# First attention: the triangle of the diagonal score blocks selected by GpSimd in SBUF instead of added by mask products in PSUM

## The chip, the cores and the metric

The kernel runs on one core of one Trainium2 chip, as one launch. The metric is the device time in microseconds of one execution; several runs are taken and their median is given. The core has five engines with a queue each that work side by side: TensorE (PE in the profile, with its weight loads listed apart as PEld), VectorE (DVE), ScalarE (ACT), GpSimd (POOL) and SyncE (SP, which here only starts DMAs). TensorE writes its results into PSUM, a small memory of eight banks; ScalarE and VectorE read them from there, and GpSimd works in SBUF, the large on-chip memory.

## The reference

The kernel computes one transformer block with two attentions and two feed-forward parts on 1024 tokens of 512 channels, in float32. The change concerns the first attention alone: 32 heads of 16 channels, rotary positions, a causal mask, and a softmax over all earlier tokens.

```python
def attention_fwd(x, wq, wk, wv, wo, n_heads=32):
    B, T, C = x.shape                       # 1, 1024, 512
    hd = C // n_heads
    xq = (x @ wq.T).reshape(B, T, n_heads, hd)
    xk = (x @ wk.T).reshape(B, T, n_heads, hd)
    xv = (x @ wv.T).reshape(B, T, n_heads, hd)
    xq = rotary_pos_emb(xq)
    xk = rotary_pos_emb(xk)
    scores = jnp.einsum('bqhd,bkhd->bhqk', xq, xk) * hd ** (-0.5)
    causal = jnp.tril(jnp.ones((T, T), dtype=bool))
    scores = jnp.where(causal[None, None], scores, NEG_INF)
    probs = jax.nn.softmax(scores.astype(jnp.float32), axis=-1).astype(xq.dtype)
    out = jnp.einsum('bhqk,bkhd->bqhd', probs, xv).reshape(B, T, C)
    return out @ wo.T

x = x + attention_a(layernorm(x))
x = x + ffn(layernorm(x))
x = x + attention_b(layernorm(x))
x = x + ffn(layernorm(x))
```

## The kernel before

The first attention lies between about 70 and 372 us of the span, after the projections of queries, keys and values. Heads are padded to 32 rows, so that four heads share the 128 partitions: one group of four heads is called a column `c` here, and there are eight (`NCA`). `qT` and `kT` hold queries and keys with channels on partitions. A score matmul of one head uses only 32 rows of the PE array, so that the matmuls of four heads can run in it at once.

For each column of heads the scores are made twice.

- **Row scores** (`row_scores`, L358): tile `s`, queries on partitions, keys along the free axis. They serve only to find each query's maximum: `maxima` (L375 and L378, VectorE) reduces them to the negated maximum, with a mask for the diagonal block added in the same instruction. `with_maxima` (L393, L397) turns the negated maxima and writes them by DMA (SP's queue) into an extra row of `qT`, where a row of ones in `kT` meets them.
- **Column scores** (`col_scores`, L407): tile `sT`, keys on partitions, queries along the free axis. Because of the extra row they come out of the matmul with the query's maximum already taken off, so that no allowed score is above zero. `exponentials` (L429, ScalarE) takes the exponential from PSUM to the SBUF tile `p`. `product` (L449) multiplies `p` with the values (and a column of ones, which yields the sums of the softmax) into the PSUM tile `oT`. `normalize` (L486 to L508) copies it out, and with several DMAs and one GpSimd multiply (L508) divides by the sums.

The work advances in steps. In step `n` of column `c`, `step` makes the column scores of column `c` and the row scores of column `c + 1`, half a step at a time: the first half takes the column scores of heads 2 and 3 with the row scores of heads 0 and 1, the second half the other way round. So each half has four score tiles. After the scores of a half come `maxima`, `exponentials`, the call `due()`, and half of the product of the step two before. A column has nine steps. The last column (`c` = 7) has no next one, and its ten steps take all four heads' column scores at once.

A step covers one score tile of 512 columns per head, put together from blocks. The blocks on the diagonal of the causal mask, where half of the entries must vanish, are gathered four at a time: `diagonal(qc)` is a list of four blocks of 128 keys by 128 queries. Each of the first seven columns has two such triangle steps, its steps 4 and 7; the last has steps 0 and 7. So there are 16 triangle steps, 14 of them in two halves. In these, `exponentials` first adds a mask of 0 and a huge negative number to the four triangles in PSUM: for each head four matmuls (L427) of a slice of the identity `identb` with the bfloat16 mask `maskT`, spread over the four blocks by a broadcast. The exponential then makes zeros of the masked entries.

Score tiles of both kinds share one PSUM pool of seven banks (`a_s`, tag `s`); the eighth is `oT`. The tiles `p` have five buffers. `later` is a list of deferred pieces of work with a count; `due()`, called once in each half-step (twice in a step of the last column), counts each down and runs those that fall below zero. Before, only `normalize` uses it, for the inversion of the sums and for L508.

The order of instructions on each engine isn't quite that of the source: a scheduler in the framework places them by its own estimate and by priorities, and assigns the buffers. Each engine then works through its queue in that order, and a waiting instruction holds up those behind it. DMAs of the first attention are issued on SP's queue; GpSimd's queue also issues some early weight loads (`midway`).

Of the kernel before, what the change touches and what calls it, by code (L numbers as in the profile page):

```python
# [10 lines left out]
BF16 = mybir.dt.bfloat16  # L11
AF = mybir.ActivationFunctionType
ALU = mybir.AluOpType
# [3 lines left out]
P = 128  # L17
# [4 lines left out]
QC = 512  # L22
# [3 lines left out]
NEG = -(2.0**100)  # L26
# [12 lines left out]
B = 32  # L39
# [25 lines left out]
class Block:  # L65
# [207 lines left out]
    def attend_a(self, ctx_pool, pt, work, ps_s, ps_o, qT, kT, v_p, project_qk, project_v, midway, tail):  # L273
        nc, tc = self.nc, self.tc
        HC = P // PADA
        with ExitStack() as ctx:
            cp = ctx.enter_context(tc.tile_pool(name="a_c", bufs=1))
# [7 lines left out]
            mask = cp.tile([P, QC], BF16, tag="mask", name="mask")  # L285
            nc.gpsimd.memset(mask, 0.0)
            nc.gpsimd.affine_select(
                out=mask, in_=mask, compare_op=ALU.is_ge, fill=NEG, base=QC - P, pattern=[[-1, QC]], channel_multiplier=1
            )
            identb = cp.tile([P, P], BF16, tag="identb", name="identb")  # L290
            make_identity(nc, identb)

            maskT = cp.tile([P, P], BF16, tag="maskT", name="maskT")
            nc.gpsimd.memset(maskT, 0.0)
            nc.gpsimd.affine_select(
                out=maskT, in_=maskT, compare_op=ALU.is_ge, fill=NEG, base=0, pattern=[[1, P]], channel_multiplier=-1
            )

# [7 lines left out]
            def diagonal(qc):  # L308
                return [(qc, 4 * qc + a, a * P, (a + 1) * P) for a in range(4)]
# [26 lines left out]
            def rows_of(j):  # L336
                return slice(j * PADA, (j + 1) * PADA)
# [11 lines left out]
            def col_pieces(c, n):  # L349
                return list(placed(by_cols(c)[n], lambda qc, b, x0, x1: x1 - x0))  # L350
# [48 lines left out]
            def col_scores(c, n, heads, made):  # L399

                pieces = col_pieces(c, n)
                masked = pieces[0][:4] in diagonal(pieces[0][0])
                for j in heads:
                    made[j] = ps_s.tile([P, QC], F32, tag="s", name=f"sT{c}_{n}_{j}")
                for x, (qc, b, x0, x1, at, end) in enumerate(pieces):
                    for j in heads:
                        nc.tensor.matmul(  # L407
                            made[j][:, at:end],
                            lhsT=kT[rows_of(j), c, b * P : (b + 1) * P],
                            rhs=qT[rows_of(j), c, qc * QC + x0 : qc * QC + x1],  # L410
                            start=x == 0,
                            stop=x == len(pieces) - 1 and not masked,
                        )
                        yield

            def exponentials(c, n, heads, made, p):
                pieces = col_pieces(c, n)
                end = pieces[-1][-1]

                if pieces[0][:4] in diagonal(pieces[0][0]):  # L420
                    mask = maskT.unsqueeze(1).to_broadcast([P, len(pieces), P])
                    for j in heads:

                        for a in range(P // B):
                            rows = slice(a * B, (a + 1) * B)
                            to = made[j][rows, :].rearrange("p (a k) -> p a k", k=P)
                            nc.tensor.matmul(to, lhsT=identb[:, rows], rhs=mask, start=False, stop=True)  # L427
                for j in heads:
                    nc.scalar.activation(p[:, j, :end], made[j][:, :end], AF.Exp)  # L429

            def product(c, n, p):

# [90 lines left out]
            later = []  # L523
# [10 lines left out]
            def step(rc, cc, n):  # L534
# [8 lines left out]
                for half in range(2 if both else 1):  # L543
                    rows, cols = (2 * half, 2 * half + 1), (2 - 2 * half, 3 - 2 * half)
                    if not both:
                        rows = cols = range(HC)
                    gens = []
                    if cc is not None:
                        gens.append(col_scores(cc, n, cols, madeT))
                    if rc is not None:  # L550
                        gens.append(row_scores(rc, n, rows, made))
                    drain(gens)
                    if rc is not None:
                        maxima(rc, n, rows, made)
                    if cc is not None:
                        exponentials(cc, n, cols, madeT, p)
                    due()
                    if not both:
                        due()
                    next(turns, None)  # L560
# [935 lines left out]
```

## Time and profile before

| | |
|---|---|
| Median of 3 runs | 1570.31 us (1570.02 to 1570.70) |
| The profiled execution's own time | 1571.58 us |
| Its span (first to last instruction) | 1569.8 us |
| Mean granted TensorE clock | 0.999 |
| Triangle mask products L427 | 256, from 132.3 to 365.3 us |
| Exponentials L429 | 292, from 120.6 to 370.4 us |
| First matmul of the output projection L1370 | 371.5 us |

A row of a costly group names the line, the engine, the operation, output and input tiles with their shapes and the count; after the bar stand the busy time in us that the group covers and the mean ns of one, and after the second bar how long the engine was idle just before them and what ended that idle time. In a listing in order of time the columns are the start in us, the duration in us, then engine, line, operation, tiles and shapes, and how many such instructions follow each other; a bracket gives the idle time before. A float32 matmul of these sizes shows as two passes. Matmuls overlap, and their ends are modelled, so that sums of PE time count overlapping parts twice where they are not given as covered time. In a table of stretches each engine's busy time is followed by the number of its instructions; then come the granted clock as a share of full speed, the busy share of the DMA engines, and GB/s.

### The profile page before, as it was taken

The numbers are of one execution on the slowest core, as the hardware profiler recorded it, in microseconds if no ns is written. First come the engines' busy times: TensorE is split into PE (matmuls) and PEld (weight loads), VectorE is DVE, ScalarE is ACT, GpSimd is POOL, SyncE is SP. The second block draws the span as 40 slices with busy tenths as digits, with TensorE's granted clock in tenths as the row PEclk, the third lists the DMA queues.
The fourth block names the chain that finished last, engine by engine and source line by source line (L and its number), as shares of the span: only waits on it lengthen the run. The fifth ranks groups of instructions, "written<-read, shape, count | busy, mean of one in ns | idle before, by whom it ended". The sixth has DMA issues, their size and how long they took to land.

```text
span 1569.8 us, 32216 instructions
## 1 busy us (share of the span) xinstructions
PE 1543.4 (98%) x12894; PEld 926.1 (59%) x12894; DVE 1058.7 (67%) x2537; ACT 662.1 (42%) x1597; POOL 463.1 (29%) x571
## 2 busy tenths in 40 slices
PE   9999999999999999999999999999999999999998
PEld 5545455555555657557656755755765675556654
DVE  4557778773566886666776667766676766776753
ACT  2216666665223544443434444343343444433430
POOL 3000000002233433432443343334244333333450
PEclk9999999999999999999999999999999999999999
DMA  5000222220033102412330331241133032135001
GB/s 208 1 1 6 20 22 19 18 20 19 29 99 95 42 1 68 68 42 55 63 60 28 82 38 31 65 72 41 54 62 61 28 69 35 34 86 122 4 2 54
DMA packets 80950, 75.34 MB, mean 48 GB/s; under 512 B 14944, under 2 KB 56672, under 8 KB 80800
## 3 DMA queue, kind: packets, MB, share of 16 engines
q1 hardware_dynamic: 70272, 52.56, 14.3%
q0 software_dynamic: 8848, 17.58, 7.7%
q10 hardware_dynamic: 1680, 3.15, 0.5%
q8 instruction: 101, 1.65, 0.5%
q14 instruction: 49, 0.40, 0.1%
HBM read 33.08 MB, written 18.87 MB: 33 GB/s over the span
## 4 chain that ended last, share of the span: by engine, by line
PE 84%; DVE 7%; POOL 4%; ACT 2%; issue 2%; SPq 0%; DMA 0%; DVEq 0%; ACTq 0%; POOLq 0%
PE s L1079 13%; PE wo L765 12%; PE o L1140 11%; PE sT L407 8%; PE pq L993 8%; PE kv L920 5%; PE oT L449 5%; PE pm_f L714 3%; PE or L1140 3%; PE s L358 3%; PE pj_v L218 2%; PE pj_q L218 2%; PE pm_ao L1370 2%; PE pj_k L218 2%; DVE p L1081 2%
## 5 line engine op out<-in xcount | busy, mean ns | idle before, releaser
L1091 POOL TENSOR_SCALAR p<-p,rs 128x1024 f32<-128x1024 f32 (+7 forms) x256 | 192.8, 754 | 407.0 <-DVE rs L1090 406.3
L1079 PE MATMUL s<-kT,qT 128*128 128x512 f32 (+3 forms) x768 | 297.0, 496 | 10.9 <-DVE p L1081 10.9
L1079 PEld LDWEIGHTS s<-kT,qT 128*128 128x128 f32 x768 | 137.9, 190 | 174.7 <-issue 114.4
L765 PE MATMUL wo<-wo,oT 128*128 128x512 f32 x512 | 237.9, 593 | 1.0 <-ACT spare L781 1.0
L1106 DVE STREAM_TRANSPOSE pT<-p 128x512 f32<-128x512 f32 (+3 forms) x256 | 152.9, 602 | 109.5 <-PE o L1140 58.8
L1088 ACT ACTIVATE p<-p,nm 128x1024 f32<-128x1024 f32 (+7 forms) x256 | 198.3, 775 | 17.9 <-ACT nm L1086 0.4
L429 ACT ACTIVATE p<-sT 128x512 f32<-128x512 f32 (+1 forms) x292 | 155.2, 593 | 89.8 <-PE s L358 35.2
L1085 DVE TENSOR_REDUCE nm<-p 128x1 f32<-128x1024 f32 (+7 forms) x256 | 188.2, 735 | 2.9
L1140 PEld LDWEIGHTS o<-pT,va 32*128 32x128 f32 x4212 | 172.9, 185 | 21.7 <-issue 10.4
L1086 ACT ACTIVATE nm<-nm 128x1 f32<-128x1 f32 x256 | 51.6, 202 | 315.6 <-DVE nm L1085 314.7
L1140 PE MATMUL o<-pT,va 32*128 32x224 f32 (+5 forms) x4212 | 181.3, 324 | 0.8 <-DVE pT L1106 0.8
L358 PE MATMUL s<-kT,qT 32*128 32x512 f32 (+3 forms) x768 | 164.4, 520 | 0.0
L407 PE MATMUL sT<-qT,kT 32*128 32x128 f32 (+3 forms) x1152 | 155.3, 401 | 0.3 <-DMA qT<-negT 0.3
L765 PEld LDWEIGHTS wo<-wo,oT 128*128 128x128 f32 x512 | 94.2, 190 | 90.7 <-issue 78.8
L1081 DVE SCALAR_TENSOR_TENSOR p<-s,rq,relr 128x512 f32<-128x512 f32 x192 | 120.9, 646 | 9.9 <-PE s L1079 9.7
L993 PE MATMUL pq<-xnTb,wq 128*128 128x512 f32 x240 | 117.8, 600 | 0.4
L1081 DVE SCALAR_TENSOR_TENSOR p<-s,rq,rel 128x512 f32<-128x512 f32 (+1 forms) x192 | 102.5, 558 | 21.0 <-PE s L1079 20.9
L407 PEld LDWEIGHTS sT<-qT,kT 32*128 32x128 f32 x1152 | 80.6, 184 | 50.6 <-issue 29.4
L1112 DVE STREAM_TRANSPOSE tT<-p 128x512 f32<-128x512 f32 (+3 forms) x128 | 63.7, 498 | 57.0 <-POOL p L1091 30.6
L375 DVE TENSOR_REDUCE part<-s 128x1 f32<-128x512 f32 x128 | 81.6, 684 | 28.1 <-PE s L358 20.1
L1090 DVE RECIPROCAL rs<-ss 128x1 f32<-128x1 f32 x256 | 39.8, 155 | 85.9 <-ACT p L1088 82.1
L508 POOL TENSOR_TENSOR o<-o,over 64x512 f32<-64x512 f32 x12 | 15.3, 1272 | 270.1 <-DMA o<-oTs 224.0
(201 smaller groups left out, 2161.8 us busy)
## 6 DMA issues: line engine op xcount, KB each, us to landing
va<-v SPq DMA_DIRECT2D x256, 64.0 KB
xd<-beside POOLq DMA_DIRECT2D x56, 256.0 KB, 4.1
wq<-in_b_WqT_dram SPq DMA_DIRECT2D x8, 1024.0 KB
wo<-in_b_WoT_dram SPq DMA_DIRECT2D x8, 1024.0 KB
x_x<-in_x_dram SPq DMA_DIRECT2D x8, 256.0 KB
wkv<-in_b_WkT_dram SPq DMA_DIRECT2D x8, 256.0 KB
xd<-x_x ACTq DMA_DIRECT2D x8, 256.0 KB
wkv<-in_b_WvT_dram SPq DMA_DIRECT2D x8, 256.0 KB
```

The costliest lines, as they stand in the source:

```text
L358: nc.tensor.matmul(made[j][:, at:end], lhsT=qT[rows_of(j), c, i * P : (i + 1) * P], rhs=kT[rows_of(j), c, kc * QC : kc * QC + end - at], s ...
L407: nc.tensor.matmul(made[j][:, at:end], lhsT=kT[rows_of(j), c, b * P : (b + 1) * P], rhs=qT[rows_of(j), c, qc * QC + x0 : qc * QC + x1], st ...
L429: nc.scalar.activation(p[:, j, :end], made[j][:, :end], AF.Exp)
L765: nc.tensor.matmul(ps, lhsT=oTs[g, h][:, t * P : (t + 1) * P], rhs=wo[:, h, :], start=(h == heads[0]), stop=(h == heads[-1]))
L993: ins = nc.tensor.matmul(ps, lhsT=w[:, kc, :], rhs=x[:, kc, :], start=first and kc == 0, stop=kc == H - 1, skip_group_check=True,)
L1079: nc.tensor.matmul(s, lhsT=qT[:, i * P : (i + 1) * P], rhs=kT[:, lo:hi], start=True, stop=True)
L1081: nc.vector.scalar_tensor_tensor(p[:, lo:hi], s, rq[:, i : i + 1], rels[i % 2][:, at + lo : at + hi], ALU.mult, ALU.add)
L1085: nc.vector.tensor_reduce(nm, p[:, :w], AX.X, ALU.max, negate=True)
L1088: nc.scalar.activation(p[:, :w], p[:, :w], AF.Exp, bias=nm, scale=slope, accum_out=ss)
L1091: nc.gpsimd.tensor_scalar(p[:, :w], p[:, :w], rs, 1.0, ALU.mult, ALU.mult)
L1106: nc.vector.transpose(PT[:, i : i + (NT - 1) * (m - 1) + 1 : NT - 1, :], p[:, : m * P].rearrange("p (j k) -> p j k", k=P))
L1140: nc.tensor.matmul(cols(o[:, a], j, j + skip), lhsT=vs[g][j // 4][rows, j % 4 * NB + b, :], rhs=moving(j, j + skip, rows, slice(b * B, (b ...
```

## The change

The mask products go, with `identb` and `maskT`. In a triangle step the scores leave PSUM by ScalarE as max(-s, 0) (`Relu` with scale -1) into `p`. GpSimd's `affine_select` then keeps the entries on and above the diagonal in SBUF and fills the others with the huge positive number, over both heads of the half (128 x 1024) or all four heads in the last column (128 x 2048). The exponential with scale -1 is taken in place in SBUF, as a deferred piece of work: its count is 1 for head 2 and 2 for the others, so that `due()` runs it in the next half-step or the one after. Steps without triangles are as before.

```diff
-            identb = cp.tile([P, P], BF16, tag="identb", name="identb")
-            make_identity(nc, identb)
-
-            maskT = cp.tile([P, P], BF16, tag="maskT", name="maskT")
-            nc.gpsimd.memset(maskT, 0.0)
-            nc.gpsimd.affine_select(
-                out=maskT, in_=maskT, compare_op=ALU.is_ge, fill=NEG, base=0, pattern=[[1, P]], channel_multiplier=-1
             )
...
             def col_scores(c, n, heads, made):
 
                 pieces = col_pieces(c, n)
-                masked = pieces[0][:4] in diagonal(pieces[0][0])
...
-                            stop=x == len(pieces) - 1 and not masked,
+                            stop=x == len(pieces) - 1,
...
             def exponentials(c, n, heads, made, p):
                 pieces = col_pieces(c, n)
                 end = pieces[-1][-1]
 
-                if pieces[0][:4] in diagonal(pieces[0][0]):
-                    mask = maskT.unsqueeze(1).to_broadcast([P, len(pieces), P])
+                if pieces[0][:4] not in diagonal(pieces[0][0]):
                     for j in heads:
-
-                        for a in range(P // B):
-                            rows = slice(a * B, (a + 1) * B)
-                            to = made[j][rows, :].rearrange("p (a k) -> p a k", k=P)
-                            nc.tensor.matmul(to, lhsT=identb[:, rows], rhs=mask, start=False, stop=True)
+                        nc.scalar.activation(p[:, j, :end], made[j][:, :end], AF.Exp)
+                    return
+
+
                 for j in heads:
-                    nc.scalar.activation(p[:, j, :end], made[j][:, :end], AF.Exp)
+                    nc.scalar.activation(p[:, j, :], made[j], AF.Relu, scale=-1.0)
+                lo, hi = min(heads), max(heads) + 1
+                of = p[:, lo:hi, :].rearrange("p j (a k) -> p (j a) k", k=P)
+                nc.gpsimd.affine_select(
+                    out=of,
+                    in_=of,
+                    compare_op=ALU.is_ge,
+                    fill=-NEG,
+                    base=0,
+                    pattern=[[0, (hi - lo) * (QC // P)], [1, P]],
+                    channel_multiplier=-1,
+                )
+                for j in heads:
+                    of = p[:, j, :]
+                    later.append([1 if j == 2 else 2, lambda of=of: nc.scalar.activation(of, of, AF.Exp, scale=-1.0)])
```

## The prediction

> **What bounds the kernel now.** I read the page's engine table, then busy time by stretch, then the first attention's costliest groups, then one triangle step in order of time, then GpSimd's rows by shape, and last the granted clock.
>
> ```profile
> PE 1543.4 (98%) x12894; PEld 926.1 (59%) x12894; DVE 1058.7 (67%) x2537; ACT 662.1 (42%) x1597; POOL 463.1 (29%) x571
> ```
>
> TensorE (PE) is busy almost throughout. A stretch inside the first attention (times are us from the span's start):
>
> ```profile
> 250.00:300.00 50.00, 50.00 (x684) 25.06 (x680) 39.86 (x110) 31.18 (x58) 3.81 (x3) 1.00 0.26 22
> ```
>
> The columns are PE, PEld, DVE, ACT, POOL, clock: PE 50.00 of 50, ScalarE (ACT) 31.18, GpSimd (POOL) 3.81. So PE sets the pace, ACT has a third of its time free, and POOL is nearly empty. What the change touches, between 80 and 520 us:
>
> ```profile
> L429 ACT ACTIVATE p<-sT 128x512 f32<-128x512 f32 (+1 forms) x292 | 155.2, 593 | 89.8 <-PE s L358 35.2 <-PE sT L427 32.5 <-PE sT L407 21.6
> L427 PE MATMUL sT<-maskT,identb 128*32 128x512 bf16 x256 | 19.3, 384 | 0.0
> ```
>
> The 256 mask products cover 19.3 us of PE. One triangle step (column 4, first triangle), PE and then ACT:
>
> ```profile
> 262.98 0.37 PE L407 MATMUL sT<-qT,kT 32*128 32x128 f32 x1
> ...
> 263.55 0.60 PE L407 MATMUL sT<-qT,kT 32*128 32x128 f32 x7
> 264.08 0.61 PE L427 MATMUL sT<-maskT,identb 128*32 128x512 bf16 x8
> 264.52 0.61 PE L449 MATMUL oT<-p,v_p 128*32 128x256 f32 x8
> 265.06 0.37 PE L407 MATMUL sT<-qT,kT 32*128 32x128 f32 x1
> ...
> 268.87 0.58 PE L407 MATMUL sT<-qT,kT 32*128 32x384 f32 x1
> ...
> 269.10 0.58 PE L358 MATMUL s<-kT,qT 32*128 32x384 f32 x1
> ...
> 270.73 0.48 PE L407 MATMUL sT<-qT,kT 32*128 32x256 f32 x1
> ```
>
> ```profile
> 264.59 1.09 ACT L429 ACTIVATE p<-sT 128x512 f32<-128x512 f32 x2 [1.21 <-PE sT L427]
> 266.70 1.08 ACT L429 ACTIVATE p<-sT 128x512 f32<-128x512 f32 x2 [1.02 <-PE sT L427]
> ```
>
> Triangle half-steps start at 262.98 and 265.06, the two halves of the next step at 267.23 and 268.87, the step after at 270.73. The masks delay the products by 264.52 - 264.08 = 0.44. ACT idles 1.0 to 1.2 before each pair.
>
> **What goes.** 28 batches of 8 masks at 0.44 and two of 16 at 0.87 (364.61 to 365.48 in the last column) are 12.3 + 1.8 = 14.1 us of PE's queue; 19.3 counts overlap with neighbours. That is the whole possible gain. The setup of `identb` and `maskT` (POOL, about 1 us near 6 to 11 us) goes too; I count nothing, since PE is 47.78 of 50 busy there behind loads and layer norm, and at most 1 us if it led.
>
> **What comes.** Relu replaces Exp at the PSUM exit, one for one; the same 128x512 ACT instruction is taken at L429's 0.60 (a copy, L486, takes 0.593). 64 Exps in place are new: two back to back occupy 1.08, so one follows another after 0.49. Bounds for an in-place Exp: 0.49 to 0.72 (L1088, 128x512 in SBUF, with a bias and a sum, 722 ns). I take 0.49, as these have neither. POOL gains 28 selects of 128x1024 and two of 128x2048, shapes the trace lacks. Its nearest rows:
>
> ```profile
> L105 POOL TENSOR_SCALAR_AFFINE_SELECT rel<-rel 128x512 f32<-128x512 f32 x2 | 1.4, 742 | 0.0
> masks.py:199 POOL TENSOR_SCALAR_AFFINE_SELECT ident<-ident 128x128 f32<-128x128 f32 x1 | 0.3, 282 | 0.0
> L1091 POOL TENSOR_SCALAR p<-p,rs 128x1024 f32<-128x1024 f32 x32 | 36.0, 1126 | 74.6 <-DVE rs L1090 74.6
> L508 POOL TENSOR_TENSOR o<-o,over 64x512 f32<-64x512 f32 x12 | 15.3, 1272 | 270.1 <-DMA o<-oTs 224.0 <-DMA over<-over 39.0 <-DMA qT<-negT 7.0
> ```
>
> The select itself: (742 - 282)/384 = 1.20 ns per element, so 0.74 + 512 x 1.20 = 1.35 at 1024 and 2.57 at 2048. Below: 1.13 (L1091). Above: L508's 2.48 ns per element, 2.54. Handing from POOL to ACT and back costs 0.12 together: at 378.04 POOL ends `mb_f`, ACT's 0.81 (L149) follows, at 378.97 POOL goes on. One round trip ACT, POOL, ACT is S = 1.35 + 0.12 = 1.47 (1.25 to 2.66).
>
> The Trainium skill (GPSIMD Engine Reference, section 3.1) gives 1.8 cycles per element at 1.2 GHz for a tight loop: by estimate 1.54 at 1024, which would add 28 x 0.19 = 5 us to the sum below.
>
> **Where the Exps stand.** The source defers them by half a step, but a scheduler lays the instructions out. In the changed program as built, ACT's queue at all 14 paired triangles reads: Relu of heads 2, 3; Exp 2, 3; Relu 0, 1; Exp 0, 1; then the next step. Each first Exp waits for a select that starts only after the Relus before it. Behind the wait on ACT's queue stand the second half's Relus and the next step's Exps, and PE waits for those, because seven PSUM banks serve all scores. As built, the fourth score matmul of the next step's second half (the one at 269.10) waits for the bank that the next step's first Exp frees (in 13 of 14 triangles; in the other a neighbour does). Its start, with 262.98 as zero: Relu starts at 1.19 (last score matmul ends 263.55 + 0.60, 0.02 to wake ACT); two Relus 1.09; S 1.47; two Exps 0.98; two Relus 1.09; S 1.47; two Exps 0.98; the next step's first Exp 0.60; 0.05 to wake PE: 8.92. From there to the step after takes 270.73 - 269.10 = 1.63: 10.55. The 14 stretches of before last 7.65 to 8.32, mean 7.77, masks included. Net 2.78 each, **38.9 us**; PE has no slack to regain it.
>
> POOL's queue: L508 stands ahead of each column's first triangle and in six columns runs across it (264.38 to 265.65, while the first select is ready at 264.17 + 1.09 + 0.08 = 265.34). It delays that select 0.2 to 0.7, together **2.6**. The DMAs of L508 and SP's queue keep their places; the 12 multiplies behind a select are needed only by the output projection. DVE keeps its instructions; at 40 of 50 it waits with PE. L508's own duration stays 1.27 to 1.28 in all 12 beside a busy DVE, so no slowdown between these two is counted.
>
> Last column (four heads at once). First triangle: Relus from 349.35 (the scores' end) on take 3 x 0.49 + 0.60 = 2.07, select 2.57 + 0.12, two Exps 0.98, four Exps of the next step 1.96, the other two Exps 1.09 (so the built order): 358.14; the products that need them take 1.08, so the next scores come at 359.2, not 355.50: +3.7. Second: the same chain from 364.65 ends at 373.44, and the last products (369.17 to 371.49, 2.32) end at 375.76: +4.3. **8.0 us**; the mask saving is inside.
>
> **The clock.** The second wait leaves PE empty: `sT1` may start at the end of the second Relu pair (1.19 + 1.09 + 1.47 + 0.98 + 1.09 = 5.82) and runs 0.58, so from 6.4 to 8.92, 2.5 us. The trace shows once what such a gap may do:
>
> ```profile
> 492.07:495.48 3.41, 1.54 (x11) 0.35 (x9) 2.01 (x3) 1.61 (x2) 0.00 (x0) 1.00 0.41 101
> 556.92:560.33 3.41, 1.65 (x14) 0.65 (x12) 3.22 (x9) 1.96 (x4) 1.49 (x2) 1.00 0.00 0
> 560.33:563.75 3.42, 3.42 (x11) 1.87 (x8) 2.61 (x9) 2.41 (x6) 1.65 (x1) 0.50 0.00 0
> ```
>
> After 3.41 us with PE 1.65 busy the granted clock was 0.50 for 3.42; after one with 1.54 it stayed. Each drop costs PE half of 3.42, 1.7. A gap of 2.5 against windows of 3.41 at any phase lies whole within one, which leaves at most 0.9 busy, in (3.41 - 2.5)/3.41, some 3 of 10 cases; of 16 gaps I take five: **8.5** (bounds 0 and 27).
>
> The Trainium skill (TensorE: Matmul & The Clock Gate, section on HAM oscillation) sets the danger at idle gaps above some 3.4 us; by it there would be no drop here and the sum would be 8.5 lower. The row at 560.33, after a gap of 1.60, differs.
>
> **The sum.** The profiled execution took 1571.58 (span 1569.8 and 1.8 around it), 1.27 above the median 1570.31. 1571.58 + 38.9 + 2.6 + 8.0 + 8.5 = 1629.6; less 1.27, **1628**.
>
> **Rivals.**
> - *Waits without clock drops* (1.54 busy once did no harm): 1628.3 - 8.5 = 1620; with the select at its lower bound, 28 x 0.22 less, 1613.
> - *A drop after nearly every gap*: 16 x 1.7 = 27, so 1647.
> - *A slow select* at L508's rate: 28 x 1.19 + 2 x 2.5 = 38 on top, 1666 with the drops. For it: L508 is slower per element; against: L105 is the same operation.
> - *Faster*: the gain stands because the waits stay off PE. ACT has 19 of 50 us free, and if the Exps really ran half a step late, four half-steps would hold 12 ACT instructions, 5.9 us against 4 x 1.64 = 6.6. Price: all of the 14.1, 1556. It decides if the round trip fits into ACT's idle 1.0 to 1.2 before each pair. S + 0.98 = 2.45 does not, and the built order doesn't defer. That is also where the change does not do what its source says.
>
> **Chances.** Forecast 0.47, no drops 0.25, many drops 0.10, slow select 0.09, faster 0.07, no change 0.02. The range 1606 to 1650 leaves out the faster cases and the slow select. About 0.2% is what a measurement here tells from no change: faster 0.07, same 0.02, slower 0.91.
>
> **What would show it.** L427 gone; ACT idle 1.4 to 1.5 before an Exp, released by POOL, about 30 times; select at 1.35; triangle start to the step after next 10.5; PE idle some 2.5 released by ACT; the first attention longer by some 50, all else unchanged; clock 0.50 in a few 3.4 us stretches. Wrong if the Exps don't wait, or PSUM holds PE up less than the built waits say.

## The result, and the profile after

| | before | after |
|---|---|---|
| Median | 1570.51 us (4 runs, 1570.02 to 1572.17) | 1650.88 us (4 runs, 1643.93 to 1654.85) |
| Ratio | | 1.0505, 95% interval 1.0465 to 1.0545 |
| The profiled execution's own time | 1571.58 us | 1653.68 us |
| Mean granted TensorE clock | 0.999 | 0.971 |
| First matmul of the output projection | 371.49 us | 454.88 us |

The changed kernel is 5% slower. The profiled execution is 82.1 us longer, and all of it arises in the first attention: its end comes 83.4 us later, and what follows takes 1.3 us less.

Line numbers move with the change: column scores are L398, row scores L350, Exp out of PSUM L413, Relu L418, the select L421, Exp in place L432, the product L452, GpSimd's multiply L511, the maxima L367 and L370.

From the page of the changed kernel: the engine table's first line, the granted clock in 40 slices (41.3 us each) and the group of the row scores.

```profile
PE 1594.6 (97%) x12638; PEld 939.8 (57%) x12638; DVE 1059.0 (64%) x2537; ACT 695.1 (42%) x1661; POOL 496.5 (30%) x597
...
PEclk9998888889899999999999999999999999999999
...
L350 PE MATMUL s<-kT,qT 32*128 32x512 f32 (+3 forms) x768 | 203.4, 588 | 25.5 <-ACT p L413 25.4
```

PE has 256 matmuls fewer and is busy 51 us longer. That can't be more work. The clock row shows one reason: slices 4 to 9 and 11, in the first attention, stand at 8. And the row scores now wait 25.4 us for ScalarE.

The stretch that was shown of before, in the same columns (PE, PEld, DVE, ACT, POOL, clock):

```profile
250.00:300.00 50.00, 46.17 (x504) 21.50 (x504) 30.90 (x92) 28.57 (x54) 6.84 (x6) 0.86 0.18 13
```

PE now has idle time here (3.83 of 50, none before), at a clock of 0.86 instead of 1.00, and does 504 matmuls instead of 684. ScalarE is busy for 28.57 us of the 50, less than the 31.18 before: it isn't the bound either. One triangle step, half after half, in ScalarE's queue in order of time (the idle time ahead and what ended it stand in brackets):

```profile
262.93 1.08 ACT L418 ACTIVATE p<-sT 128x512 f32<-128x512 f32 x2 [0.89 <-PE s L350]
265.41 1.15 ACT L432 ACTIVATE p<-p 128x512 f32<-128x512 f32 x2 [1.39 <-POOL p L421]
266.46 1.06 ACT L418 ACTIVATE p<-sT 128x512 f32<-128x512 f32 x2
268.72 1.15 ACT L432 ACTIVATE p<-p 128x512 f32<-128x512 f32 x2 [1.19 <-POOL p L421]
269.77 1.06 ACT L413 ACTIVATE p<-sT 128x512 f32<-128x512 f32 x2
```

and GpSimd's queue beside it:

```profile
263.07 1.26 POOL L511 TENSOR_TENSOR o<-o,over 64x512 f32<-64x512 f32 x1 [21.71 <-DMA o<-oTs]
264.29 1.08 POOL L421 TENSOR_SCALAR_AFFINE_SELECT p<-p 128x1024 f32<-128x1024 f32 x1
267.60 1.09 POOL L421 TENSOR_SCALAR_AFFINE_SELECT p<-p 128x1024 f32<-128x1024 f32 x1 [2.22 <-ACT p L418]
```

Relu, wait, Exp, Relu, wait, Exp: the Exp that the source defers stands directly behind the Relus of its own half, and ScalarE sits idle 1.39 and 1.19 for GpSimd. Only at 269.77 can it empty a bank for the next step. TensorE's matmuls and, in the last line, its weight loads:

```profile
267.58 0.91 PE L398 MATMUL sT<-qT,kT 32*128 32x384 f32 x2
270.40 0.62 PE L350 MATMUL s<-kT,qT 32*128 32x384 f32 x1 [1.92 <-ACT p L413]
...
272.03 1.08 PE L452 MATMUL oT<-p,v_p 128*32 128x256 f32 x8
```

```profile
270.40 0.18 PEld L350 LDWEIGHTS s<-kT,qT 32*128 32x128 f32 x1 [2.53 <-ACT p L413]
```

PE is empty for 1.92 us, its loader for 2.53, until that bank is free. Then the product of the next lines takes 1.08 where a product of the same eight matmuls took 0.61 before. The windows of the granted clock around this gap (the last but two column is the clock):

```profile
263.99:267.40 3.41, 3.41 (x49) 1.92 (x47) 2.63 (x11) 2.02 (x5) 1.39 (x2) 1.00 0.25 13
267.40:270.82 3.42, 1.50 (x13) 0.60 (x10) 0.86 (x6) 2.23 (x5) 1.09 (x1) 1.00 0.84 26
270.82:274.23 3.41, 3.41 (x27) 1.91 (x26) 1.71 (x8) 1.10 (x3) 1.27 (x1) 0.50 0.02 1
274.23:277.64 3.41, 3.41 (x44) 2.00 (x36) 1.59 (x8) 1.09 (x2) 0.00 (x0) 0.50 0.02 5
277.64:281.06 3.42, 3.42 (x68) 2.31 (x62) 2.99 (x13) 2.17 (x4) 0.00 (x0) 1.00 0.00 0
```

After the window with the gap (PE 1.50 of 3.42), two whole windows run at half clock, although PE is shown busy throughout in both. The trace has 15 such stretches between 141 and 455 us, 13 of them two windows long, 95.6 us at half clock together.

Two costs, then: a wait and a slower clock. A triangle's length, from its start to the start of the step after next, is 7.77 on average before. The first triangle after the change, which ends just as the first half-clock stretch begins (141.1), takes 10.28; the others but one take 11.1 to 12.6 (the exception, 8.34, is column 6's first, where PE's gap is only 0.50). The excess of the 14 is 49.3, the last column's 12.6, and the other 21 to 22 lie mostly in half-steps behind the triangles that run at the low clock.

### The profile page after: what moved, and what is told of

It is laid out like the page before. It is cut to its first block, busy times and chain, and to the rows that moved or that the text cites. A ratio compares the mean times of both kernels' runs of the same rounds, so it can differ in the third digit from the quotient of the medians.

```text
span 1651.9 us, 31785 instructions
## 1 busy us (share of the span) xinstructions
PE 1594.6 (97%) x12638; PEld 939.8 (57%) x12638; DVE 1059.0 (64%) x2537; ACT 695.1 (42%) x1661; POOL 496.5 (30%) x597
## 4 chain that ended last, share of the span: by engine, by line
PE 58%; DVE 7%; POOL 3%; ACT 2%; issue 2%; DVEq 0%; ACTq 0%; POOLq 0%
PE s L1082 12%; PE wo L768 11%; PE o L1143 10%; PE pq L996 7%; PE kv L923 5%; PE pm_f L717 3%; PE or L1143 3%; PE pm_ao L1373 2%; DVE p L1084 2%; POOL p L1094 2%; DVE pT L1109 1%; PE st L1060 1%; DVE nm L1088 1%; ACT p L1091 1%; DVE oT L1192 1%
## 5 line engine op out<-in xcount | busy, mean ns | idle before, releaser
L350 PE MATMUL s<-kT,qT 32*128 32x512 f32 (+3 forms) x768 | 203.4, 588 | 25.5 <-ACT p L413 25.4
L398 PE MATMUL sT<-qT,kT 32*128 32x128 f32 (+3 forms) x1152 | 192.4, 451 | 4.4 <-ACT p L413 4.4
L413 ACT ACTIVATE p<-sT 128x512 f32<-128x512 f32 (+1 forms) x228 | 120.5, 589 | 83.0 <-PE s L350 62.2
L398 PEld LDWEIGHTS sT<-qT,kT 32*128 32x128 f32 x1152 | 93.9, 205 | 65.9 <-issue 31.4
L350 PEld LDWEIGHTS s<-kT,qT 32*128 32x128 f32 x768 | 85.4, 211 | 48.9 <-ACT p L413 34.4
L367 DVE TENSOR_REDUCE part<-s 128x1 f32<-128x512 f32 x128 | 81.8, 686 | 43.0 <-PE s L350 37.7
L452 PE MATMUL oT<-p,v_p 128*32 128x128 f32 (+1 forms) x1552 | 106.0, 377 | 1.4 <-ACT p L432 1.4
```

The costliest lines, as they stand in the source:

```text
L350: nc.tensor.matmul(made[j][:, at:end], lhsT=qT[rows_of(j), c, i * P : (i + 1) * P], rhs=kT[rows_of(j), c, kc * QC : kc * QC + end - at], s ...
L398: nc.tensor.matmul(made[j][:, at:end], lhsT=kT[rows_of(j), c, b * P : (b + 1) * P], rhs=qT[rows_of(j), c, qc * QC + x0 : qc * QC + x1], st ...
```

## The experiments

Each kernel was timed beside runs of the kernel before (medians 1570.04 to 1570.71); ratios are to these.

**1. The Exps really half a step late.** The deferred Exps are pinned to where the source puts them, nothing else is changed.

```diff
-                    later.append([1 if j == 2 else 2, lambda of=of: nc.scalar.activation(of, of, AF.Exp, scale=-1.0)])
+                    later.append([1 if j == 2 else 2, lambda of=of: tc.keep_in_program_order(
+                        nc.scalar.activation(of, of, AF.Exp, scale=-1.0))])
```

> The changed kernel with its deferred Exps pinned to the place the source gives them, so that ScalarE's queue reads Relu 2, 3; Relu 0, 1; Exp 2; two Exps of the next step; Exp 3; two more; Exp 0, 1. Nothing is left out. My theory (the loss is the wait for GpSimd in ScalarE's queue, plus the clock that falls in the gaps it makes): the 41 us of ScalarE waiting for GpSimd and the low clock disappear; 14 us of mask products are saved, some 8 us come back where the products of a triangle tile wait for Exps 0 and 1, which stand last, and some 4 us in the last column: 1560 to 1575 us. Rival 1 (the 64 extra Exps are too much for ScalarE, wherever they stand): above 1600. Rival 2 (GpSimd's select in SBUF slows the other engines): above 1600, with longer instructions on VectorE or ScalarE.

Measured: 1577.57 (1576.82 to 1578.36), ratio 1.0046 (1.0032 to 1.0060). Of the 80 us, 73 are gone with every Relu, select and Exp still there. ScalarE's queue in the same place (L435 is the Exp in place here), and once in the last column:

```profile
262.25 1.08 ACT L418 ACTIVATE p<-sT 128x512 f32<-128x512 f32 x2 [0.83 <-PE s L350]
264.64 1.08 ACT L418 ACTIVATE p<-sT 128x512 f32<-128x512 f32 x2 [1.30 <-PE s L350]
265.61 0.63 ACT L435 ACTIVATE p<-p 128x512 f32<-128x512 f32 x1
...
350.74 0.63 ACT L435 ACTIVATE p<-p 128x512 f32<-128x512 f32 x1 [2.11 <-POOL p L421]
```

The second Relu pair no longer stands behind a wait, and the triangles are 4.45 us shorter in sum than before the change. So the extra load of ScalarE and GpSimd is not what costs; the place of the Exps in ScalarE's queue is. Nor are the instructions of ScalarE and VectorE longer in the changed kernel: an Exp out of PSUM takes 595 ns on average before and 593 after, the first maxima on VectorE (L375, then L367) 685 and 686 (between 120 and 345 us). The time still missed its range, by 2.6: in the last column, where one select covers four heads, the wait for GpSimd is still there, with two half-clock stretches behind it (353.4 and 373.9), and that column is 9.45 us longer than before.

**2. The wait kept, the gap filled.** 32 small bfloat16 matmuls into a part of a score tile that is written over afterwards, just ahead of the matmul that waits for the bank.

```diff
+            few = cp.tile([P, P], BF16, tag="few", name="few")
...
+                        if c and n in (5, 8) and heads == (2, 3) and j == 3 and at == 0 and len(pieces) == 2:
+                            for _ in range(32):
+                                over = made[2][:, end : end + P]
+                                tc.keep_in_program_order(nc.tensor.matmul(over, lhsT=few, rhs=few, start=True, stop=True))
```

> The changed kernel with 32 small bfloat16 matmuls (128 columns, into a part of a score tile that is overwritten right after) put on TensorE's queue just where it stands still, in 13 of the 14 paired triangles. They need no buffer and do nothing for the result. My theory (two losses: the wait itself, and a clock that falls because TensorE stood still): the waits stay, the granted clock stays at 1.0 outside the last column, and some 78 of 96 us at half clock go, so about 39 us: 1605 to 1618 us. Rival (the clock falls for another reason than the gap): no faster than the changed kernel, 1650 or, with the added matmuls, more.

Measured: 1619.09 (1616.02 to 1619.39), ratio 1.0304 (1.0290 to 1.0318), just above its range. The page's clock row and the place of the gap in PE's queue:

```profile
PEclk9999999998999999999999999999999999999999
```

```profile
264.82 0.91 PE L405 MATMUL sT<-qT,kT 32*128 32x384 f32 x2
265.66 1.96 PE L356 MATMUL s<-few 128*128 128x128 bf16 x32
267.64 0.58 PE L357 MATMUL s<-kT,qT 32*128 32x384 f32 x1
```

The waiting matmul starts about as late as with the gap, but the clock stays at full speed in all 13 places where the gap is filled. Three half-clock stretches are left, 6.8 each: from 369.0, behind column 6's first triangle, and from 392.9 and 413.3 in the last column, all in places where nothing was filled in. The first of them fits the account badly:

```profile
365.55:368.96 3.41, 2.91 (x22) 1.52 (x22) 1.29 (x2) 2.22 (x5) 1.09 (x1) 1.00 0.67 28
368.96:372.37 3.41, 3.41 (x30) 2.05 (x29) 1.38 (x2) 2.17 (x5) 1.26 (x1) 0.50 0.00 0
```

PE's only gap there is 0.50 and its window shows 2.91 busy, yet a drop follows; in the changed kernel the same place, with a gap of 0.50 and a window of 3.09, has none. So filling a gap removes its drop, but PE's busy time in this profile doesn't say everything that the clock goes by. Thirteen triangles now take 10.26 to 10.72 and one (column 6's first) 8.15, 34.9 us more than before in sum: that is nearly the wait alone. The 31.8 us between this kernel and the changed one are the clock's share that the filler takes away.

**3. No select.** Relu and Exp in place stay where the scheduler puts them; GpSimd's select between them is left out.

```diff
-                lo, hi = min(heads), max(heads) + 1
-                of = p[:, lo:hi, :].rearrange("p j (a k) -> p (j a) k", k=P)
-                nc.gpsimd.affine_select(
...
-                )
```

> The changed kernel without GpSimd's select: its triangles are not masked, all 64 Relus and 64 extra Exps stay, in the same places on ScalarE's queue. My theory: without the round trip to GpSimd the chain from the first Relu to the first Exp of the next step is 2 x (1.1 + 1.05) + 0.6 = 4.9 us, no longer than the pair of steps took with masks, so that TensorE hardly waits and its clock stays: 1562 to 1576 us. Rival 1 (ScalarE's extra work is the loss): above 1600 us.

Measured: 1569.87 (10 runs), ratio 0.9997 (0.9988 to 1.0006), as expected. ScalarE's queue (L421 is the Exp in place here):

```profile
262.76 1.08 ACT L418 ACTIVATE p<-sT 128x512 f32<-128x512 f32 x2 [1.02 <-PE sT L398]
263.73 1.15 ACT L421 ACTIVATE p<-p 128x512 f32<-128x512 f32 x2
```

The Exps stand behind the Relus of their half as in the changed kernel, but without a round trip, and there is no half-clock stretch in the first attention. So the whole loss hangs on the trip to GpSimd and back, in this order of the queue. It also says that the rest of the change, 256 masks less and 64 Exps more, comes out even.

**4. Masks gone, nothing in their place.** Only the Relu is left in a triangle step: select and Exp in place are left out.

```diff
...
-                nc.gpsimd.affine_select(
...
-                for j in heads:
-                    of = p[:, j, :]
-                    later.append([1 if j == 2 else 2, lambda of=of: nc.scalar.activation(of, of, AF.Exp, scale=-1.0)])
```

> The changed kernel with only the Relu left in the triangle steps: no select and no Exp there, so the triangles are neither masked nor exponentiated. It shows what the mask products alone cost. My theory: 14.1 us less than the kernel before, 1554 to 1559 us. Rival (VectorE or the banks bound the triangle steps, so that the masks were partly hidden): 1562 to 1570 us.

Measured: 1562.28 (1561.32 to 1562.39), ratio 0.9946 (0.9932 to 0.9959). The masks are worth 8, not 14; the rival's range held. Compared with the run before, the 64 Exps cost 1569.87 - 1562.28 = 7.6 in their place. Where the other 6 are: on average over columns 1 to 5, the first half-step of a triangle goes from 2.07 to 1.67, but the second only from 2.19 to 2.16 (first triangle of a column) and from 2.08 to 1.88 (second). PE's weight loads in such a second half, then VectorE at the same time:

```profile
259.64 0.18 PEld L398 LDWEIGHTS sT<-qT,kT 32*128 32x128 f32 x1
260.07 0.18 PEld L350 LDWEIGHTS s<-kT,qT 32*128 32x128 f32 x1 [0.24 <-DVE neg L370]
```

```profile
259.37 0.64 DVE L370 CUSTOM_DVE_ANT_0 junk<-s,mask,part 128x512 f32<-128x512 f32 x1
259.94 0.07 DVE L370 DVE_READ_ACCUMULATOR2_ANT neg<- 128x1 f32 x1
259.94 0.73 DVE L370 CUSTOM_DVE_ANT_0 junk<-s,mask,part 128x512 f32<-128x512 f32 x1
...
260.69 0.75 DVE L370 CUSTOM_DVE_ANT_0 junk<-s,mask,part 128x512 f32<-128x512 f32 x1
```

The fourth score tile needs a bank that VectorE's maxima have to free, and VectorE works without a pause there. The mask products had lain partly over this wait.

**5. The same with short maxima.** As experiment 4, and in the row scores' steps 4 and 7 the maxima read 64 columns instead of all; the other Exps get a scale of 0.001.

```diff
-                        s, w = made[j][:, at:end], end - at
+                        w = 64 if c and n in (4, 7) else end - at
+                        s = made[j][:, at : at + w]
...
```

> As e5_masks_gone (only the Relu in the triangle steps), and in the row scores' steps 4 and 7 VectorE reads 64 columns of each tile instead of 512, so that its maxima there are partial; the other Exps have a small scale. It asks whether VectorE is why taking the masks away gave 8.2 us and not 14.1. My theory (the fourth score matmul of a triangle's second half waits for VectorE's maxima): the missing 4 to 6 us come, 1556 to 1559 us. Rival (the masks only hid TensorE's own change from score to product matmuls): as e5, 1561 to 1563.

Measured: 1556.70 (1556.36 to 1556.95), ratio 0.9914 (0.9900 to 0.9927), as expected. With VectorE out of the way most triangles fall to 6.83 to 6.90 and the gain is 1570.04 - 1556.70 = 13.3, close to the masks' 14.1. So VectorE was the cover for most of the missing part. The kernel before with short maxima and masks was not run; but its triangles, 108.75 in sum, are only 1.65 longer than 14 times the shortest (7.65), so that by estimate at most some 1.7 of the 13.3 could have been had there too.

**6. The select over one head of two.** Head 3 (or 1) of each half is left unselected; shape 128x512 instead of 128x1024, in the last column two heads of four.

```diff
-                lo, hi = min(heads), max(heads) + 1
+                lo, hi = min(heads), min(heads) + len(heads) // 2
```

> The changed kernel with the select over the first half of the heads alone, so 128x512 in a half-step and 128x1024 in the last column; the triangles of the other heads stay unmasked. It makes the same waits shorter, about 0.6 instead of 1.09 for the select, so each paired triangle's chain by 2 x 0.49 = 0.98 us, and the stand of TensorE from 1.9 to some 0.9 us. My theory (a 3.41 us stretch with less than about 1.7 us of TensorE work drops the clock): no drops at the paired triangles, and of the 34.9 us of waits 14 x 0.98 = 13.7 go: 1590 to 1602 us with low clock only in the last column. Rival (any wait drops the clock, whatever its length): 1625 or more.

Measured: 1574.49 (1574.05 to 1575.81), ratio 1.0028 (1.0017 to 1.0039): far below what I expected. ScalarE's queue:

```profile
266.39 1.09 ACT L418 ACTIVATE p<-sT 128x512 f32<-128x512 f32 x2 [1.02 <-PE sT L398]
267.51 0.63 ACT L432 ACTIVATE p<-p 128x512 f32<-128x512 f32 x1
268.52 0.63 ACT L432 ACTIVATE p<-p 128x512 f32<-128x512 f32 x1 [0.38 <-POOL p L421]
269.06 1.06 ACT L418 ACTIVATE p<-sT 128x512 f32<-128x512 f32 x2
270.15 1.15 ACT L432 ACTIVATE p<-p 128x512 f32<-128x512 f32 x2
```

I had halved only the select (0.63 instead of 1.09). It also starts after one Relu instead of two, and the scheduler puts the unselected head's Exp ahead, which fills the wait: ScalarE idles 0.38 and 0 instead of 1.39 and 1.19. PE's longest gap between 120 and 345 us is 0.61, no half-clock stretch follows any, and the triangles cost 4.6 in sum instead of 49.3. ScalarE's wait, shorter by about one us, twice, is worth 76 us of the 80. The loss doesn't shrink in proportion to the wait: of the 49.3 in the triangles 4.6 are left, and the half clock is gone. How much of this the shorter select does, and how much the other order, this run doesn't separate.

**7. The select last.** Relu and Exp one after the other, pinned, the second of them half a step later, then the select with zeros as fill, so that PE's product, not ScalarE, waits for GpSimd. The last column keeps its mask products.

```diff
-                    later.append([1 if j == 2 else 2, lambda of=of: nc.scalar.activation(of, of, AF.Exp, scale=-1.0)])
...
+                exp(lo)
+                later.append([1, lambda: (exp(lo + 1), select())])
```

> Nothing left out. Another order in the 14 paired triangles: Relu, Exp at once and without a wait (the second Exp of a pair half a step later), GpSimd's select last, filling zeros; mask products kept in the last column. ScalarE never waits for GpSimd, TensorE's product needs the select only two steps later. My theory: as the one before, 1561 to 1568 us. Rival (ScalarE's extra load): 1569 or more.

Measured: 1612.28 (1611.93 to 1613.92), ratio 1.0270 (1.0256 to 1.0284), a plain miss. GpSimd's queue at one of the columns (L534 is the multiply, L444 the select):

```profile
253.86 1.25 POOL L534 TENSOR_TENSOR o<-o,over 64x512 f32<-64x512 f32 x1 [7.48 <-DMA over<-over]
255.08 2.13 POOL L444 TENSOR_SCALAR_AFFINE_SELECT p<-p 128x1024 f32<-128x1024 f32 x2
```

The scheduler laid the multiply of the column before, which waits 7.48 for its DMA, ahead of two selects that were ready. In six columns the half-step of the product that needs them takes 6.6 to 7.5 instead of 1.65, and a half-clock stretch follows each time. What the idea is worth without that queue can't be read here: the triangles, disturbed ones among them, are 3.4 longer than before in sum. It is the same mistake on another queue: an engine that works in order, with a waiting instruction ahead of a ready one.

**8. Exps spread evenly.** Pinned as in experiment 1, with counts 1, 1, 1, 2 for heads 2, 3, 0, 1; mask products as before in the last column.

```diff
-                    later.append([1 if j == 2 else 2, lambda of=of: ...])
+                    later.append([2 if j == 1 else 1, lambda j=j: later_exp(j)])
```

> Nothing left out. The 14 paired triangles as in the change, but the Exps are pinned one half-step later (heads 2, 3 and 0) and two (head 1), so that ScalarE's queue reads Relu 2, 3; Relu 0, 1, Exp 2, 3; two Exps of the next step, Exp 0; two more, Exp 1; the last column keeps its mask products. My theory (the masks cost 8 us of the pace, the waits are gone, the last column's extra ScalarE work was what e1 lost): 1561 to 1567 us, faster than the kernel before. Rival (ScalarE's 56 extra Exps still hold up TensorE): 1568 or more.

Measured: 1570.58 (11 runs), ratio 1.0000 (0.9992 to 1.0009); the rival's range held. The weight loads in the second half of the step after a triangle (L359 are the row scores, L431 the Exp out of PSUM):

```profile
268.06 0.18 PEld L408 LDWEIGHTS sT<-qT,kT 32*128 32x128 f32 x1
268.60 0.18 PEld L359 LDWEIGHTS s<-kT,qT 32*128 32x128 f32 x1 [0.35 <-ACT p L431]
```

Two Relus and two Exps stand ahead of the Exp that frees the bank, so that this half-step takes 2.29 and 2.68 (first and second triangle, on average over columns 1 to 5) instead of 1.91 and 1.86.

**9 and 10. Experiment 1 with mask products in the last column, and the Exps of heads 3 and 1 both two half-steps late.** Counts 1, 2, 2, 2 for heads 2, 3, 0, 1, then 1, 2, 1, 2; the lines stand against those of experiment 8.

```diff
-                    later.append([2 if j == 1 else 1, lambda j=j: later_exp(j)])
+                    later.append([1 if j == 2 else 2, lambda j=j: later_exp(j)])     (9)
+                    later.append([2 if j in (1, 3) else 1, lambda j=j: later_exp(j)])     (10)
```

> The half-step-late kernel, but the last column keeps its mask products and its Exps straight out of PSUM as before the change. The half-step-late kernel took 1577.57, of which its last column was 9.45 us longer than before and its 14 paired triangles 4.45 us shorter. If the two are independent: 1577.6 - 9.45 = 1568.1, so 1566.5-1569.5, ratio 0.997 to 0.9995, with paired triangles again 4 to 5 us shorter in sum and the last column within 0.5 of 23.3. Rival (the shorter triangles were only the other side of the last column's clock drops, or the 56 extra Exps come due elsewhere): 1570 or more, ratio 1.000 or above.

> As the half-step-late kernel with masks kept in the last column, but heads 2 and 0 get their Exp one half-step later and heads 3 and 1 two half-steps later. The two half-steps after the triangle then hold at most four ScalarE instructions each, and none of them four ahead of the bank that the fourth score matmul needs. If the lateness of a bank behind four ScalarE instructions in one half-step is what the evenly spread kernel paid (1570.6), this one gives 1565-1569. Rival (any place for 56 extra Exps costs about what the masks did): 1569.5-1572.

Measured, 11 runs each beside 21 of before (median 1570.71): 1569.23 (1567.66 to 1570.58), ratio 0.9987 (0.9978 to 0.9996), and 1568.96 (1568.28 to 1571.30), ratio 0.9990 (0.9981 to 0.9999). In 9 the triangles are again 4.5 shorter in sum and the last column takes 22.97 against 23.29, as the sum of the two parts said; in 10 the triangles are 1.4 shorter. The time of 10 lies in its range, but not for the reason given: all its second triangles but the last take 8.03, longer than the 7.89 of experiment 8, and the half-step that was slow there (2.68) takes 2.70. Both intervals lie below 1, but by 0.1% at the middle, which is less than the 0.2% that I had set for telling a difference from none. If the difference is real, these two stand ahead of the kernel before by 1.5 to 1.8 us. With the masks worth 8.0 (experiment 4) and 56 Exps to be paid from that, little more is to be had in this way.

## Why the prediction was right in direction and short in size

The forecast of 1628 had the sign, the place and the mechanism; 1650.88 lies 0.88 above the upper end of its range, 1606 to 1650. The steps in turn, with the 82.1 us of the profiled execution split up as the runs allow:

| | predicted | measured |
|---|---|---|
| Waits in the 14 paired triangles, masks taken off, with the multiply ahead of the select | 38.9 + 2.6 = 41.5 | 34.9 (experiment 2) |
| Waits in the last column | 8.0 | 4.9 to 12.6 |
| Half clock | 8.5 | the rest: 35 to 42 |

*The built order.* Right, and it was the heart of it. Relu, Exp, Relu, Exp at the triangles, ScalarE waiting for GpSimd 30 times, 40.7 us in all, 1.36 each (forecast 1.4 to 1.5). The view of the longest waits of the changed kernel between 120 and 455 us (engine, what it waited for, us in total, times, longest):

```profile
ACT p L432 <- POOL p L421: 40.7, 30, 2.1
...
PEld s L350 <- ACT p L413: 34.4, 15, 2.5
```

Experiment 1 shows that it is the order: pinned to the source's place, the wait in the paired triangles goes.

*The chain through the PSUM bank.* Right in kind: in 13 of the 14 paired triangles the fourth score matmul waits for the next step's first Exp. TensorE's own gap there is 1.92, though, not the forecast 2.5, because the score matmuls before it run until 267.58 + 0.91 = 268.49; only its loader stands for 2.53. From the first Relu to that matmul it takes 270.40 - 262.93 = 7.47, against 8.92 - 1.19 = 7.73 forecast; the first triangle's length is 10.28 against 10.55.

*The select.* Sized too long: 1.35 worked out from L105, 1.09 measured, below even the 1.13 taken as the lower end. At 128x2048 it is 2.005 instead of 2.57.

```profile
L421 POOL TENSOR_SCALAR_AFFINE_SELECT p<-p x30: 1082/1091/2005, 133.3 to 444.3; 128x1024 f32<-128x1024 f32 x28, 128x2048 f32<-128x2048 f32 x2
```

Put in the sum, 41.5 - 28 x 0.26 = 34.2, close to the 34.9 of experiment 2. Part of that closeness is luck: column 6's first triangle hardly waits (8.15 in experiment 2), and the other 13 exceed the mean of before by 2.65 each, more than 34.2/14 = 2.44. The slow select as a rival falls with the same row, and the Trainium skill's figure for a loop (GPSIMD Engine Reference, section 3.1), 1.54 by estimate, is further off still.

*The in-place Exp.* Two take 1.15, one after 0.52 instead of 0.49: right.

*The last column.* Its length grew by 12.6, and 15.4 us of it ran at half clock. If all of that halved PE's work, 7.7 is the clock's and 4.9 the wait's; idle parts of it cost nothing, so the wait is 4.9 or more. The 8.0 can't be told from it.

*The clock.* This is the term that was mis-sized, by a factor of four to five, in the paragraph on the clock: "A gap of 2.5 against windows of 3.41 at any phase lies whole within one [...] of 16 gaps I take five", at "1.7" each. Three things were wrong in it.

First the count: 15 gaps were followed by a drop, not five of 16; the sixteenth place, column 6's first triangle, had a gap of only 0.50. In part the condition was too strict. A gap didn't have to lie whole within one window and leave 0.9 busy: the row of before that the forecast rests on had 1.65 busy. By that row 1.76 of a gap of 2.5 would have been enough, which at any phase happens in (3.41 + 2.5 - 2 x 1.76)/3.41, some 7 of 10 cases, 11 of 16. Two of the 15 gaps do reach across the edge of a window (the first triangles of columns 0 and 1), and a drop followed all the same:

```profile
137.70:141.11 3.41, 1.66 (x22) 0.87 (x22) 0.65 (x3) 2.81 (x6) 0.04 (x1) 1.00 0.00 0
178.66:182.07 3.41, 1.70 (x7) 0.81 (x6) 1.20 (x8) 2.22 (x5) 1.09 (x1) 1.00 0.92 31
```

Second, the phase was not random. The other 13 gaps, 1.92 long (2.14 and 2.21 in the last column), lie whole within a window, where any phase would give (3.41 - 1.92)/3.41, 4 of 10. Behind the first triangles of columns 1 to 5 the gap begins 1.70, 1.29, 1.08, 1.44 and 1.29 after the start of a window: from one such triangle to the next it takes 44.1 to 44.9, close to thirteen windows of 3.413 (44.37), so that each gap falls near the place of the one before.

Third, the length: a drop lasted not one window but, in 13 of 15 stretches, two, which costs 3.4 us instead of 1.7. Half of the 95.6 us is 47.8 as an upper bound; 35 to 42 is what the other rows leave. The upper bound of 27 that I had set held the count, not the length. Experiment 2 shows the clock's part directly, by 31.8 us in the places that it fills.

The Trainium skill's rule that was weighed in the prediction (TensorE: Matmul & The Clock Gate, section on HAM oscillation: danger at idle gaps above some 3.4 us) would have had no drop at all; here gaps of 1.92 between matmuls did it, and the measurement decides.

*The rivals.* "A drop after nearly every gap", 1647 at a chance of 0.10, came closest, partly by luck: its count was right and its price per drop half, while its waits were too long by about 7. Waits without drops is what experiment 2 comes near to, 1619.09 against 1620, and that it lies so near also owes to the three stretches left in it. "Faster" was priced wrongly twice. If the Exps are really late there is a gain, but not 14.1: 8.0 with nothing in the masks' place, as VectorE's maxima lie beneath the masks (experiments 4 and 5), and 1.5 to 1.8 at best with the Exps paid for (9 and 10). And its condition, that the round trip has to fit into ScalarE's idle 1.0 to 1.2, isn't needed: experiment 1 has the round trip beside other work, and its triangles are shorter than before.

What stays open: why a stretch is two windows nearly always; why a drop followed the window with 2.91 busy in experiment 2, and none the one with 1.54 in the kernel before; and whether the nearness of the column's length to thirteen windows comes by chance or is made by the drops themselves. No run here separates these.

## What to carry to other kernels

Read the built queue of every engine that works in order before believing that a piece of work is deferred: an instruction that waits for another engine costs what stands behind it, and pinning the work half a step later was worth 73 us here. Where the bound engine would fall idle, price the gap twice, as a wait and as what the clock does afterwards, and don't assume random phase in a loop with a fixed period. Before counting a removed instruction at its full time, look for what waits next in that same half-step; here 6 of 14 us were not gained, most of them for another engine's work beneath the masks.

## What the hardware showed that I had not expected

- A gap of 1.92 us between matmuls (PE 1.50 to 1.70 busy in its window of 3.41) was followed by half clock all 13 times, and 13 of the 15 drops of the changed kernel lasted 6.83 us. Where no gap of PE was longer than 0.62 (experiments 1 and 6, between 120 and 345 us) there was no half clock, and 1.96 us of small matmuls in the gap kept the clock at full speed. One drop in experiment 2 came after a gap of 0.50, so this is not a threshold.
- The changed kernel's executions differ by up to 11 us, and the clock accounts for it in the two compared here: 1653.68 at 0.971 (span 1651.9) and 1643.93 at 0.977 (span 1642.2). At half clock for the rest, 2 x 0.029 x 1651.9 = 95.8 and 2 x 0.023 x 1642.2 = 75.5; half of the difference is 10.1, the times differ by 9.75.
- GpSimd's in-place select took 0.63, 1.09 and 2.005 at 512, 1024 and 2048 elements per partition, 0.9 ns per element, where the 128x512 one on `rel` had taken 0.742.
